# Reading the strided operand on TensorE instead of PSUM on VectorE: the closes of images 1 to 3 of a state-space and attention block

## The chip, the cores and the metric

The kernel runs on one core of one Trainium2 chip. The metric is the device time of a run in microseconds. Before the change three runs took 6413.48, 6416.27 and 6428.01 us, a median of 6416.27 us.

## The reference

The input is four images of 96 channels and 128x128 pixels. Two layers follow each other, each of the form x + layer(groupnorm(x)).

Layer 0 is a state-space block: a projection to 192 channels, a depthwise 3x3 convolution, four scans over the pixels (by rows, by columns, and both backwards), a norm, and a projection back to 96 channels.

Layer 1, in which the change lies, is an attention convolution:

```
xr, x1, x2 = relu_split_norm(x)             # the positive and the negative half, each normalised
y1 = layer_norm(attn_conv(x1, x2))          # softmax(key x query) gives 3x3 weights for each image
y2 = layer_norm(conv3x3(x2, w_conv2)) * x1
out = xr + conv1x1(concat(y1, y2), w_full) + b_full
```

The last line is what the text calls the **close** of an image. Two products of 96x96 with the pixels of the image, one for y1 (called `o` in the kernel) and one for y2 (called `c2`), are summed, and `xr` with the layer's residual (called `e`) is added. The norms are folded in: `o` carries a row of ones for the shift, and `c2` has its mean subtracted and is multiplied by `x1` on VectorE before the product.

## The kernel before

**Stages.** First the state-space block runs for all images, in part beside image 0's layer 1. Then images 0 to 3 go through layer 1 one after the other. `attention` is the convolutions of one image (helpers `products` and `outputs`: matmuls at L1477 and L1492, copies out of PSUM on ScalarE at L1550, combinations on VectorE at L1564 to L1572). Beside the convolutions of image b runs the lighter work: the norm and the splitting of image b+1, and the close of image b-1. Image 3 has nobody after it, so its close is cut up in the class `LastOutput`: `before` prepares `x1` and `e` early, `beside` adds the product of `c2` and `e` into an SBUF tile `kept` beside image 3's own last convolution, and `after` adds the product of `o` at the very end and stores.

**The order of the work.** Python generators yield an estimated cost after each piece, and `co_run` interleaves two of them by these costs: the attention on the left, the lighter chain on the right. The order in which instructions are emitted so is the order on each engine's queue; each engine waits on semaphores for its operands. The costs yielded are constants in the code and do not depend on how long an instruction takes on the chip.

**Two orders of pixels.** Image 0 goes through layer 1 with its pixels in the plain order (row by row); in the code it is `mapped`. Images 1 to 3 are kept with every row of 128 pixels cut into four sets of every fourth pixel (32 each), since their convolution works on such planes. The result has to leave in plain order, so each close of images 1 to 3 must turn it somewhere. Two views of a row do that: `pixels(v)` (L2292) reads a tile of planes in pixel order, so that its last dimension has 4 elements at a step of 32 words; `plain(v)` (L2296) is a tile in pixel order, contiguous, written with the same dimensions.

**The close.** In `attn_output` (L2299) a step is 8 rows of the image, 1024 pixels, 16 steps an image. In a step the tiles `o`, `c2` and `xx` come from DRAM; ScalarE and VectorE make `x1` and `e` (L2283 to L2290), VectorE scales `c2` (L2326), and for each of two halves of 512 pixels TensorE does two matmuls into one PSUM bank (L2334 and L2335), and VectorE adds `e` and writes the output tile (L2337 for image 0, contiguous; L2339 for images 1 and 2, with PSUM and `e` read by `pixels`). The tile is stored by a DMA on SyncE's queue at L2341. `beside` has the same with one matmul (L2412) and the addition at L2413. In `after`, one addition at L2440 takes 1024 pixels from two PSUM banks and adds into `kept` in place; its matmuls are at L2436, its store at L2443, and all 16 steps of it follow the last convolution, with nothing else left to do.

Of the kernel before, what the change touches and what calls it, by code (L numbers as in the profile page):

```python
# [20 lines left out]
CH = 512  # L21
# [50 lines left out]
def kernel(  # L72
# [26 lines left out]
    nc = tc.nc  # L99
# [236 lines left out]
    def traced():  # L336
        return nc.cur_bb.bb.instructions

    def in_order(first):


        before = {}
        for i in traced()[first:]:
            if i.engine in before:
                tc.add_manual_dep(
                    i,
                    before[i.engine].name,
                    mybir.DependencyInfo(
                        mybir.DependencyClass.NoSync, mybir.DependencyReason.DATA
                    ),  # L350
                    reason="order of emission",
                )
            before[i.engine] = i
# [56 lines left out]
    def image_stats(b, pool):  # L410
# [17 lines left out]
        return mv, run  # L428

    def project(b, weights, mv, beside, zb, xrows, ps):  # L430


# [1019 lines left out]
    def pairs_of(ps):  # L1452

        return ps.tile([128, 2, CH], F32, name="two", tag="two")
# [804 lines left out]
    def own_weights(img, ps, pool):  # L2259

        so, _ = combine(ps, img.ost.rearrange("p c s -> p (c s)"), mean96, "so")
        ro = col("ro")
        rsqrt(ro, so[:, 1:2])
        w1 = pool.tile([128, C], F32, name="w1")
        nc.vector.tensor_scalar(w1[0:C], wful[:, 0], ro, None, ALU.mult)
        nso = col("nso")
        nc.vector.tensor_scalar(nso, so[:, 0:1], -1.0, None, ALU.mult)
        pt = bank(ps)[C : C + 1, 0:C]  # L2270
        nc.tensor.matmul(pt, lhsT=img.keep["low"][:, 1:2], rhs=ident, start=True, stop=False)
        nc.tensor.matmul(pt, lhsT=nso, rhs=w1[0:C], start=False, stop=True)  # L2272
        nc.vector.tensor_copy(w1[C : C + 1], pt)
        return w1[0 : C + 1]

    def with_ones(pool, name, bufs=None):
        y = pool.tile([128, SN], F32, name=name, tag=name, bufs=bufs)
        nc.gpsimd.memset(y[C : C + 1], 1.0)
        return y[0 : C + 1]

    def first_half(img, xx, x1):
        thr, scale, shift = (img.keep[n] for n in ("thr", "scale", "shift"))
        nc.scalar.activation(x1, xx, AF.Identity, scale=scale[:, 0:1], bias=shift[:, 0:1])  # L2283
        nc.vector.scalar_tensor_tensor(x1, xx, thr, x1, ALU.is_gt, ALU.mult)

    def residual(img, xx, e):
        up, low, thr = (img.keep[n] for n in ("up", "low", "thr"))
        nc.scalar.activation(e, xx, AF.Identity, scale=up[:, 0:1], bias=up[:, 1:2])
        nc.vector.scalar_tensor_tensor(e, xx, thr, e, ALU.is_gt, ALU.mult)
        nc.vector.scalar_tensor_tensor(e, xx, low[:, 0:1], e, ALU.mult, ALU.add)  # L2290

    def pixels(v):  # L2292

        return v.rearrange("p (h j t) -> p h t j", j=TW, t=TN)

    def plain(v):  # L2296
        return v.rearrange("p (h t j) -> p h t j", j=TW, t=TN)

    def attn_output(img, ps, side, share):  # L2299
        ob = out[img.b].rearrange("c h w -> c (h w)")  # L2300
        with (
            tc.tile_pool(name="f1", bufs=1, side=side) as p1,
            tc.tile_pool(name="f3", bufs=2, side=side) as p3,
        ):
            w1 = own_weights(img, ps, p1)
            s2, w2 = c2_weights(img, ps, p1)
            ones = [with_ones(p1, f"o{i}") for i in range(2)]

            def loads(t):
                o = ones[t % 2]  # L2310
                got = [o]
                nc.sync.dma_start(o[0:C], img.od[:, bass.ts(t, SN)])
                for name, src in (("c2", img.c2d), ("xx", img.xnew)):
                    y = p3.tile([C, SN], F32, name=name)
                    nc.sync.dma_start(y, src[:, bass.ts(t, SN)])
                    got.append(y)
                return got

            ahead = loads(0)
            for t in range(NS):  # L2320
                o, c2, xx = ahead
                if t + 1 < NS:
                    ahead = loads(t + 1)
                x1 = p3.tile([C, SN], F32, name="x1")
                first_half(img, xx, x1)
                nc.vector.scalar_tensor_tensor(  # L2326
                    c2, c2, s2[0:C, 0:1], x1, ALU.subtract, ALU.mult
                )
                e = p3.tile([C, SN], F32, name="e")
                residual(img, xx, e)  # L2330
                for h in range(2):
                    sl = bass.ts(h, CH)
                    pf = part(ps, C, CH)
                    nc.tensor.matmul(pf, lhsT=w1, rhs=o[:, sl], start=True, stop=False)  # L2334
                    nc.tensor.matmul(pf, lhsT=w2, rhs=c2[:, sl], start=False, stop=True)  # L2335
                    if img.mapped:
                        nc.vector.tensor_add(x1[:, sl], pf, e[:, sl])  # L2337
                    else:
                        nc.vector.tensor_add(plain(x1[:, sl]), pixels(pf), pixels(e[:, sl]))  # L2339
                    yield 2.6 * share  # L2340
                nc.sync.dma_start(ob[:, bass.ts(t, SN)], x1)  # L2341

    class LastOutput:
# [38 lines left out]
        def beside(self):  # L2382

            img = self.img
            while self.kept is None:
                yield None
            with (
                tc.tile_pool(name="f1", bufs=1, side=self.side) as p1,
                tc.tile_pool(name="f3", bufs=2, side=self.side) as p3,
            ):  # L2390
                s2, w2 = c2_weights(img, self.ps, p1)

                def loads(t):
                    got = []
                    for name, src in (("c2", img.c2d), ("x1", self.x1d), ("e", self.ed)):
                        y = p3.tile([C, SN], F32, name=name)
                        nc.sync.dma_start(y, src[:, bass.ts(t, SN)])
                        got.append(y)
                    return got

                ahead = loads(0)
                for t in range(NS):
                    c2, x1, e = ahead
                    if t + 1 < NS:
                        ahead = loads(t + 1)
                    nc.vector.scalar_tensor_tensor(
                        c2, c2, s2[0:C, 0:1], x1, ALU.subtract, ALU.mult
                    )
                    for h in range(2):
                        sl = bass.ts(h, CH)  # L2410
                        pf = part(self.ps, C, CH)
                        nc.tensor.matmul(pf, lhsT=w2, rhs=c2[:, sl], start=True, stop=True)  # L2412
                        nc.vector.tensor_add(  # L2413
                            plain(self.kept[:, t, sl]), pixels(pf), pixels(e[:, sl])
                        )
                        yield 2.2

        def after(self, pairs):

            img, ob = self.img, out[self.img.b].rearrange("c h w -> c (h w)")  # L2420
            with (
                tc.tile_pool(name="f1", bufs=1, side=self.side) as p1,
                tc.tile_pool(name="f3", bufs=6, side=self.side) as p3,
            ):
                here = (H - OWN) // RS
                loaded = []
                for t in range(here):
                    o = with_ones(p3, "o")
                    nc.sync.dma_start(o[0:C], img.od[:, bass.ts(t, SN)])
                    loaded.append(o)  # L2430
                w1 = own_weights(img, self.ps, p1)
                for t in (*range(here, NS), *range(here)):
                    o = loaded[t] if t < here else self.own[0 : C + 1, bass.ts(t - here, SN)]
                    pf = pairs_of(pairs)[:C]
                    for h in range(2):
                        nc.tensor.matmul(  # L2436
                            pf[:, h], lhsT=w1, rhs=o[:, bass.ts(h, CH)], start=True, stop=True
                        )
                    to = self.kept[:, t]
                    nc.vector.tensor_add(  # L2440
                        plain(to), pixels(pf.rearrange("p h w -> p (h w)")), plain(to)
                    )
                    nc.sync.dma_start(ob[:, bass.ts(t, SN)], to)  # L2443
                    yield 2.6

# [252 lines left out]
```

## Time and profile before

| What | Value |
|---|---|
| median of 3 runs | 6416.27 us |
| profiled execution, its own time | 6409.68 us |
| its span in the profile | 6407.8 us |
| mean granted TensorE clock | 0.902 |
| DMA, mean over the span | 188 GB/s |
| close of image 1: VectorE's additions at L2339 | 5461 to about 5672 us |
| close of image 2: the same | about 5680 to 5907 us |
| image 3, `beside`: additions at L2413 | 6205 to 6349 us |
| image 3, `after`: matmuls at L2436 | 6366 to 6397 us |

One execution was profiled. The span counts from the first to the last event of the profile, and the execution's own time is 1.9 us longer. "PE" is TensorE's matmul, "PEld" its loading of weights, which overlaps; "DVE" is VectorE, "ACT" ScalarE, "POOL" GpSimd. A matmul of f32 in the code is two instructions of each kind in the profile. The matmuls are pipelined, so the duration of one includes its latency, and two in a row start closer together than they last. A row of a group has the line in the kernel, engine, operation, output and inputs, shapes and count, and then the busy time and the mean of one in ns, or the minimum, median and maximum.

### The profile page before, as it was taken

The page shows a single profiled execution, that of the slowest core. Times are in us where ns is not written, and L with a number is a line of the kernel's source. Part 1 is how long each engine was busy: PE and PEld are TensorE (multiplying, and loading weights), DVE is VectorE, ACT ScalarE, POOL GpSimd, SP SyncE. Part 2 cuts the span into 40 slices and gives each one's busy share as a digit, 9 for nine tenths or more (in the row PEclk, how much of TensorE's full clock was granted, in tenths as well). Part 3 has the DMA queues.
Part 4 walks back from the last instruction along what each step waited for, and adds up shares of the span by engine and source line. Part 5 has one row for each costly group of instructions (what it writes and reads, how often), then busy time and mean ns, then how long its engine had stood idle before and what let it go on. Part 6 is the DMA issues. An engine that isn't in the chain of part 4 may idle for free. (4 is left out here: it accounts for less than half of the span.)

```text
span 6407.8 us, 76468 instructions
## 1 busy us (share of the span) xinstructions
PE 5253.4 (82%) x23264; PEld 2254.8 (35%) x23264; DVE 4699.9 (73%) x7132; ACT 3759.4 (59%) x4770; POOL 3238.6 (51%) x2476
## 2 busy tenths in 40 slices
PE   6889988987888643989988588977888877889888
PEld 2333322322222111444433234345333444345553
DVE  4247878988989768989844686468774687988767
ACT  1247767787787666777622465466644665545642
POOL 1326757978879554979822234436304365022310
PEclk9899989998999765999999799989989888999989
DMA  6766777775675766676667686665776656967668
GB/s 155 175 160 189 198 199 199 214 221 163 198 202 171 202 183 207 196 213 179 182 185 195 166 228 163 195 169 156 214 199 184 175 149 165 245 167 180 191 168 221
DMA packets 897706, 1205.30 MB, mean 188 GB/s; under 512 B 230644, under 2 KB 745642, under 8 KB 884816
## 3 DMA queue, kind: packets, MB, share of 16 engines
q1 hardware_dynamic: 866640, 1145.36, 65.5%
q0 software_dynamic: 16336, 38.51, 2.3%
q10 hardware_dynamic: 14320, 16.54, 0.9%
q8 instruction: 187, 3.06, 0.2%
q14 instruction: 223, 1.83, 0.1%
HBM read 777.82 MB, written 345.62 MB: 175 GB/s over the span
## 5 line engine op out<-in xcount | busy, mean ns | idle before, releaser
L633 PE MATMUL bank<-y,wp 128*128 128x512 f32 (+3 forms) x3584 | 1310.9, 622 | 83.8 <-DMA y<-y 41.0
L866 POOL TENSOR_TENSOR y<-y,dl 128x1024 f32<-128x1024 f32 x384 | 1058.5, 2757 | 263.0 <-DVE dl L858 240.3
L833 POOL TENSOR_TENSOR dl<-dl,u 128x1024 f32<-128x1024 f32 x384 | 1008.8, 2627 | 253.1 <-ACT dA L809 121.1
L854 DVE TENSOR_TENSOR_SCAN dA<-dA,pBC 128x512 f32<-128x512 f32 x768 | 981.6, 1278 | 30.7
L2169 PE MATMUL bank<-y,wn 128*64 128x384 f32 (+5 forms) x2408 | 680.1, 507 | 58.3 <-DMA y<-x1d 34.1
L1477 PE MATMUL two<-ya,wd 128*64 128x192 f32 (+3 forms) x2376 | 582.2, 414 | 174.0 <-ACT odd L1550 65.1
L633 PEld LDWEIGHTS bank<-y,wp 128*128 128x128 f32 (+3 forms) x3584 | 456.2, 168 | 749.3 <-issue 651.1
L858 DVE TENSOR_TENSOR dl<-dA,pBC 128x512 f32<-128x512 f32 x768 | 528.5, 688 | 255.8 <-PE pBC L747 183.8
L747 PE MATMUL pBC<-xr,wbc 60*128 60x512 bf16 (+1 forms) x1536 | 457.8, 404 | 311.5 <-DVE dA L854 239.1
L1938 ACT COPY yb<-ya 64x768 f32<-64x768 f32 (+1 forms) x660 | 537.7, 815 | 195.5 <-PE two L1477 113.8
L676 ACT ACTIVATE dl<-pd,dtb 128x512 f32<-128x512 f32 x768 | 485.5, 684 | 187.9 <-PE pd L747 171.5
L1477 PE MATMUL two<-yb,wd 128*64 128x192 f32 (+3 forms) x2376 | 559.0, 400 | 4.0 <-ACT yb L1938 4.0
L837 DVE TENSOR_TENSOR pBC<-dl,pBC 128x512 f32<-128x512 f32 x768 | 527.5, 687 | 8.8 <-POOL dl L833 7.8
L2169 PEld LDWEIGHTS bank<-y,wn 128*64 128x64 f32 (+3 forms) x2408 | 310.3, 169 | 357.2 <-issue 186.2
L809 ACT ACTIVATE dA<-dl,negA 128x1024 f32<-128x1024 f32 x384 | 420.3, 1141 | 2.3
L1477 PEld LDWEIGHTS two<-ya,wd 128*64 128x64 f32 (+1 forms) x2376 | 262.2, 165 | 370.9 <-ACT odd L1550 75.0
L676 ACT ACT_TABLE_LOAD x248 | 318.2, 1283 | 91.9 <-PE pd L747 79.7
L747 PEld LDWEIGHTS <-wbc 60*128 60x128 bf16 (+1 forms) x1536 | 103.1, 96 | 752.1 <-issue 739.3
L1477 PEld LDWEIGHTS two<-yb,wd 128*64 128x64 f32 (+1 forms) x2376 | 289.7, 167 | 150.5 <-issue 42.1
L1477 PE MATMUL two<-ya,wa 128*96 128x384 f32 (+1 forms) x528 | 231.2, 521 | 72.9 <-DMA ya<-vp 27.0
L1550 ACT COPY odd<-two 128x384 f32<-128x384 f32 (+5 forms) x176 | 115.8, 658 | 291.3 <-PE two L1492 179.1
L1406 POOL TENSOR_TENSOR pl<-x 96x256 f32<-96x256 f32 (+3 forms) x396 | 275.2, 710 | 0.0
(322 smaller groups left out, 9105.4 us busy)
## 6 DMA issues: line engine op xcount, KB each, us to landing
u<-zb SPq DMA_DIRECT2D x192, 1024.0 KB
yms<-y SPq DMA_DIRECT2D x96, 512.0 KB
xn<-xnew SPq DMA_DIRECT2D x128, 384.0 KB
ya<-vp SPq DMA_DIRECT2D x120, 336.0 KB
y<-y SPq DMA_DIRECT2D x128, 258.2 KB
zb<-z SPq DMA_DIRECT2D x64, 512.0 KB
y<-yms SPq DMA_DIRECT2D x64, 512.0 KB
ya<-x1p SPq DMA_DIRECT2D x90, 336.0 KB
```

The source lines that it names most:

```text
L633: nc.tensor.matmul(blocks(pz[p:e]), lhsT=ws[k][:, d, c : c + e - p], rhs=window(ys[k], at, d, n), start=(i == 0), stop=(i == len(terms) - 1),)
L676: nc.scalar.activation(dst, src, AF.Softplus, bias=bias)
L747: nc.tensor.matmul(p, lhsT=w[rows], rhs=xr[rows, at : at + CH], start=True, stop=True)
L809: nc.scalar.activation(live[m]["dA"], live[m]["dl"], AF.Exp, scale=negA[:, g % 3, k : k + 1])
L833: nc.gpsimd.tensor_mul(t, t, u_view(n))
L837: nc.vector.tensor_mul(p, live[n]["dl"][:, bass.ts(half, CH)], p)
L854: nc.vector.tensor_tensor_scan(h, h, p, init, ALU.mult, ALU.add)
L858: nc.vector.tensor_mul(live[n]["dl"][:, sl], live[n]["dA"][:, sl], live[n]["C", half])
L866: nc.gpsimd.tensor_add(v, v, t.rearrange("p (a b) -> p a b", b=W))
L1477: nc.tensor.matmul(of(to[p:e], r), lhsT=w[:, i, c : c + e - p], rhs=tiles(t[k][PAIR[i]][:, SLOT[i]], o, r), start=(k == 0), stop=False,)
L1938: nc.scalar.copy(yb[k][64 * h - 64 : 64 * h, :, :n], ya[k][0:64, :, h * TN : h * TN + n])
L2169: nc.tensor.matmul(pc[p:e, :n].rearrange("p (h w) -> p h w", w=W), lhsT=w[:, c : c + e - p], rhs=v[:, :, 0:W], start=(i == 0), stop=(i == ...
```

## The change

In the closes of images 1 to 3, the matmuls now read their moving operand (`o` and `c2`, in SBUF) through `pixels`, so that the product stands in PSUM in pixel order. VectorE's addition then reads PSUM through `plain`, in contiguous rows. `e` is still read through `pixels` at L2339 and L2413. In `after`, `kept` is in pixel order already, so the addition becomes contiguous in all its operands and needs no view. Image 0 and everything before the closes stay as they were, and so do the counts of instructions, the tiles, their buffers, the waits and the transfers.

```diff
@@ attn_output
                     pf = part(ps, C, CH)
-                    nc.tensor.matmul(pf, lhsT=w1, rhs=o[:, sl], start=True, stop=False)
-                    nc.tensor.matmul(pf, lhsT=w2, rhs=c2[:, sl], start=False, stop=True)
+                    to, in_order = pf, lambda v: v
+                    if not img.mapped:
+                        to, in_order = plain(pf), pixels
+                    nc.tensor.matmul(to, lhsT=w1, rhs=in_order(o[:, sl]), start=True, stop=False)
+                    nc.tensor.matmul(to, lhsT=w2, rhs=in_order(c2[:, sl]), start=False, stop=True)
                     if img.mapped:
                         nc.vector.tensor_add(x1[:, sl], pf, e[:, sl])
                     else:
-                        nc.vector.tensor_add(plain(x1[:, sl]), pixels(pf), pixels(e[:, sl]))
+                        nc.vector.tensor_add(plain(x1[:, sl]), plain(pf), pixels(e[:, sl]))
@@ LastOutput.beside
-                        nc.tensor.matmul(pf, lhsT=w2, rhs=c2[:, sl], start=True, stop=True)
+                        nc.tensor.matmul(
+                            plain(pf), lhsT=w2, rhs=pixels(c2[:, sl]), start=True, stop=True
+                        )
                         nc.vector.tensor_add(
-                            plain(self.kept[:, t, sl]), pixels(pf), pixels(e[:, sl])
+                            plain(self.kept[:, t, sl]), plain(pf), pixels(e[:, sl])
                         )
@@ LastOutput.after
                         nc.tensor.matmul(
-                            pf[:, h], lhsT=w1, rhs=o[:, bass.ts(h, CH)], start=True, stop=True
+                            plain(pf[:, h]), lhsT=w1, rhs=pixels(o[:, bass.ts(h, CH)]),
+                            start=True, stop=True,
                         )
                     to = self.kept[:, t]
-                    nc.vector.tensor_add(
-                        plain(to), pixels(pf.rearrange("p h w -> p (h w)")), plain(to)
-                    )
+                    nc.vector.tensor_add(to, pf.rearrange("p h w -> p (h w)"), to)
```

## The prediction

> **What bounds the kernel now.** I read the page first, then the groups by line and shape, then the chain of waits, then busy time by stage, then single instructions in order of time. The page's head says TensorE is the busiest engine and VectorE the next; neither is at its limit over the whole span, so the change has to be priced in the stages that it touches.
>
> ```profile
> span 6407.8 us, 76468 instructions
> PE 5253.4 (82%) x23264; PEld 2254.8 (35%) x23264; DVE 4699.9 (73%) x7132; ACT 3759.4 (59%) x4770; POOL 3238.6 (51%) x2476
> ```
>
> Those stages, in the view of busy time by stage (columns: stretch and length, busy time and instructions of PE, PEld, DVE, ACT, POOL, granted clock, DMA share, GB/s), are the close of image 1, the close of image 2, image 3's half with `w2`, and image 3's last half:
>
> ```profile
> 5455.00:5675.00 220.00, 193.97 (x672) 83.30 (x672) 191.26 (x260) 108.91 (x129) 8.79 (x15) 0.93 0.81 219
> 5675.00:5908.00 233.00, 212.25 (x1202) 113.57 (x1198) 193.40 (x264) 110.93 (x134) 68.85 (x84) 0.97 0.69 178
> 6203.00:6349.00 146.00, 135.63 (x425) 55.41 (x426) 111.19 (x157) 59.63 (x74) 0.06 (x1) 0.95 0.86 222
> 6366.00:6398.00 32.00, 31.12 (x64) 11.34 (x64) 19.10 (x17) 0.00 (x0) 5.68 (x6) 0.89 0.68 205
> ```
>
> TensorE is busy 88%, 91%, 93% and 97% of them, VectorE 87%, 83%, 76% and 60%. So here TensorE leads, with VectorE close behind only in image 1's close. The chain of waits ends with the last half, and it is all TensorE:
>
> ```profile
> 6365.90 0.28 DVE w L2273
> 6366.18 0.04 issue
> 6366.23 31.13 PE two L2436 x64
> 6397.36 0.02 issue
> 6397.38 1.22 DVE e L2440
> ```
>
> **VectorE's price of a stride.** One row for each of the forms concerned (minimum, median and maximum ns, first and last start):
>
> ```profile
> L2337 DVE TENSOR_TENSOR x<-bank,e x32: 677/684/689, 4654.1 to 4777.2; 96x512 f32<-96x512 f32 x32
> L2339 DVE TENSOR_TENSOR x<-bank,e x64: 1010/1034/1084, 5461.2 to 5905.8; 96x512 f32<-96x512 f32 x64
> L2440 DVE TENSOR_TENSOR e<-two,e x16: 1221/1221/1221, 6370.0 to 6397.4; 96x1024 f32<-96x1024 f32 x16
> L1570 DVE TENSOR_TENSOR two<-ends,two 96x768 f32<-96x768 f32 x40 | 38.3, 957 | 1.1
> ```
>
> L2337 is the addition with everything contiguous, L2339 the same with PSUM and the SBUF operand `e` both read at a step of 32 words, L2440 with PSUM alone at that step. L1570 takes 957 ns for rows of 768, and 555 ns in its form of 128x384: 1.047 ns an element and 153 ns fixed. A contiguous row of 1024 would then take 1225 ns; L2440 takes 1221. So the PSUM step costs VectorE nothing here, and the 350 ns that L2339 has over L2337 (0.68 ns an element, 1.73 ns in all) belong to `e`, which the change leaves as it is.
>
> **TensorE's pace.** In the last half, in order of time, three loads of weights in a row:
>
> ```profile
> 6387.31 0.16 PEld L2436 LDWEIGHTS two<-o,w 97*96 97x96 f32 x1 [0.27 <-issue]
> ...
> 6387.74 0.16 PEld L2436 LDWEIGHTS two<-o,w 97*96 97x96 f32 x1 [0.27 <-issue]
> 6388.17 0.16 PEld L2436 LDWEIGHTS two<-o,w 97*96 97x96 f32 x1 [0.27 <-POOL o L2278]
> ```
>
> Steady matmuls start 0.43 us apart: 512 columns at 0.84 ns. (The 592 ns of a row is one matmul's length with its latency; the starts are what counts.) Each f32 matmul of the code is two such instructions: L2436 has 64 for 16 steps of 2.
>
> [...]
>
> **The change part by part.** No instruction is added, removed or moved, no DMA changes, no wait is added, and the tiles and their buffers stay. Only the length of existing instructions can change.
>
> VectorE: 64 additions at L2339 and 32 at L2413 lose the step on PSUM and keep it on `e`. Worth 0 by L2440[...], 350 ns each (33.6 us) if, against L2440, the whole excess were PSUM's. [...] The 16 at L2440 become contiguous: 1221 to 1225, nothing. A loss is excluded, since all three streams are at most as scattered as now.
>
> TensorE: in images 1 and 2, 16 steps x 2 halves x 2 matmuls x 2 instructions = 128 each, 256 in all (L2334, L2335); 64 at L2412; 64 at L2436. None of the trace's matmuls moves an operand one word at a time, so the cost is bounded. Below: 0 [...] I take the price that SBUF charges VectorE for exactly this pattern, 1.73 ns a word: 886 ns against 428, +458 each. That is an estimate, carried over from another engine.
>
> TensorE time: 256 x 0.458 = 117 us in the closes; 64 x 0.458 = 29 us at L2412; at L2436 the first 8 instructions start 0.85 us apart, at half the clock, where 1.66 ns a word is the pace anyhow, so 56 x 0.458 = 26 us. Sum 172 us.
>
> What is on the path: in the two closes TensorE is idle 26 and 21 us, part of it latency at the ends of bursts; I let half, 23 us, absorb. Behind a slow matmul stand the convolution's matmuls of the next image in the same queue, and behind those ScalarE's copies and VectorE's combinations, so the rest shows: +94. At L2412 half of 10 us idle absorbs: +24. In the last half nothing hides: +26. But the stores there are behind already:
>
> ```profile
> 6386.00:6396.00 10.00, 10.00 (x25) 3.85 (x24) 7.03 (x7) 0.00 (x0) 1.33 (x2) 1.00 0.94 300
> 6396.00:6400.00 4.00, 1.34 (x4) 0.22 (x2) 2.11 (x2) 0.00 (x0) 0.00 (x0) 1.00 0.95 299
> 6400.00:6404.00 4.00, 0.00 (x0) 0.00 (x0) 0.00 (x0) 0.00 (x0) 0.00 (x0) 0.55 0.95 290
> ```
>
> The DMA engines are full for 20 us, the last addition ends at 6398.6, its store is issued only at 6401.4, and the span ends at 6407.8. A slower TensorE lets that queue run dry and the last store goes at once: about 4 us back, +22 net. Sum +140[...]. The profiled execution took 6409.7 us (span 6407.8), so 6549; the median of the runs lies 6.6 above it, so 6555.
>
> **The rivals.**
> - *TensorE reads the step for free.* For it: the transposes at L1770 load their weights from the ring at a step of 3 words, and lone words cost nothing there: ten in a row take 0.90 us, or 0.083 us for 90 columns, 0.92 ns a word against VectorE's 1.73. [...] It decides if the starts stay 0.43 us apart.
> - *A part of the price.* [...]
> - *A dearer step*[...]
> - *Faster: TensorE reads for free and VectorE's excess was PSUM's.* 96 x 0.35 = 33.6 us of VectorE; where it is the second-busiest engine some half would show, 17 us: 6399. L2440 speaks against it. It decides from 13 us saved, 135 ns an addition.
>
> **How the numbers follow.** A measurement of this kernel tells about 0.2%, 12.8 us, from no change. Chances: full price 0.50, part 0.14, dearer 0.07, free 0.25, faster 0.04. So slower 0.71, same 0.25, faster 0.04. The likeliest is 6555, by itself 6520 to 6590 (absorption of none or of all idle time, a price of 1.6 to 1.8 ns). The range must reach the free case and leaves out the dearer one, the faster one and edges: 6408 to 6590.
>
> **What would show it.** Right: L2334, L2335, L2412 and L2436 start 0.85 to 0.9 us apart in bursts; the last half grows from 31 to about 57 us; the closes are about 47 us longer each; VectorE's L2339 and L2413 stay between 1015 and 1035 ns, L2440 at 1221; the stores after the last addition end sooner than 9.2 us. Wrong: starts still 0.43 us apart (free), or L2339 near 684 ns (the excess was PSUM's)[...]. If the starts double and the closes hardly lengthen, the absorption is what I mis-sized: VectorE, or the DMA at 0.81 of its capacity in image 1's close, would then have been the bound.

## The result and the profile after

The changed kernel takes 6569.57 us, the median of four runs (6567.35 to 6580.81), against 6414.88 us before (four runs, one more than in the table above). The ratio is 1.0247 with a 95% interval of 1.0229 to 1.0266: slower by 155 us between the medians, by 158 us by the ratio. The profiled execution has a span of 6565.5 us, 157.7 more than the one of before, so the two traces can be compared stretch by stretch.

The page of the kernel after, its head:

```profile
span 6565.5 us, 76455 instructions
PE 5449.6 (83%) x23264; PEld 2286.2 (35%) x23264; DVE 4705.9 (72%) x7132; ACT 3765.0 (57%) x4770; POOL 3237.1 (49%) x2476
```

TensorE is busy 196 us longer with the same number of instructions. VectorE, for whose sake PSUM is now read in rows, is busy 6 us longer. The forms that answer to those of before (minimum, median and maximum in ns; L2338 was L2335 and holds image 0's close too, L2342 was L2339, L2415 was L2412, L2418 was L2413, L2441 was L2436, L2446 was L2440):

```profile
L2338 PE MATMUL bank<-c,w x192: 590/1047/1169, 4649.6 to 6011.0; 96*96 96x512 f32 x192
L2415 PE MATMUL bank<-c,w x64: 1032/1048/1093, 6310.6 to 6479.2; 96*96 96x512 f32 x64
L2441 PE MATMUL two<-o,w x64: 1047/1047/1167, 6504.0 to 6558.9; 97*96 97x512 f32 x64
L2342 DVE TENSOR_TENSOR x<-bank,e x64: 1010/1031/1085, 5461.2 to 6012.1; 96x512 f32<-96x512 f32 x64
L2418 DVE TENSOR_TENSOR e<-bank,e x32: 1010/1028/1052, 6312.7 to 6480.3; 96x512 f32<-96x512 f32 x32
L2446 DVE TENSOR_TENSOR e<-two,e x16: 1219/1221/1221, 6507.8 to 6560.0; 96x1024 f32<-96x1024 f32 x16
```

A matmul with the strided operand lasts 1047 ns where it lasted 592, and VectorE's additions have lost 3 to 7 ns of 1035, or nothing. The distance from one start to the next is shorter than that length: in the last half, in order of time, the loads of weights now start 0.87 us apart instead of 0.43:

```profile
6540.68 0.26 PEld L2441 LDWEIGHTS two<-o,w 97*96 97x96 f32 x1 [0.61 <-issue]
6541.55 0.26 PEld L2441 LDWEIGHTS two<-o,w 97*96 97x96 f32 x1 [0.61 <-issue]
6542.42 0.26 PEld L2441 LDWEIGHTS two<-o,w 97*96 97x96 f32 x1 [0.61 <-issue]
```

This half alone would not tell the price of the step from that of the clock, which was 0.50 throughout: before the change the contiguous matmuls at half the clock started 0.85 us apart as well. L2415 tells it. In its stretch the clock averaged 0.89, and not one of its 64 matmuls took less than 1032 ns, where the median before was 592 ns at 0.94.

The chain of waits ends as before with TensorE's last half, 56.02 us instead of 31.13:

```profile
6503.99 56.02 PE two L2441 x64
6560.01 0.02 issue
6560.03 1.22 DVE e L2446
```

Where the 157.7 us lie is seen by cutting both traces at the same three instructions: the first addition of image 1's close, the first matmul beside image 3's convolution, and the first matmul of the last half. The first of them starts at 5461.2 us in both traces. Busy time by stretch (length, then PE, PEld, DVE, ACT, POOL, clock, DMA share, GB/s), of before:

```profile
5461.00:6204.00 743.00, 651.87 (x3733) 357.83 (x3731) 586.88 (x887) 382.22 (x471) 166.34 (x239) 0.94 0.71 190
6203.90:6366.20 162.30, 142.39 (x457) 59.13 (x456) 124.54 (x187) 62.91 (x81) 5.41 (x6) 0.94 0.82 214
6366.20:6407.80 41.60, 31.12 (x64) 11.34 (x64) 19.54 (x16) 0.00 (x0) 5.68 (x6) 0.83 0.69 209
```

and of after:

```profile
5461.00:6310.60 849.60, 775.92 (x3732) 374.86 (x3730) 588.92 (x886) 382.11 (x470) 165.56 (x239) 0.90 0.62 166
6310.60:6504.00 193.40, 177.16 (x458) 63.46 (x457) 125.13 (x187) 62.85 (x81) 5.41 (x6) 0.89 0.70 180
6504.00:6565.50 61.50, 55.99 (x64) 16.22 (x64) 19.53 (x16) 0.00 (x0) 5.68 (x6) 0.50 0.48 141
```

The stretches grow by 106.6, 31.1 and 19.9 us. In the first, image 1's close (its last addition starts at 5652 us before, not at 5672, and at 5698 us after) is 46 us longer and image 2's 61. Two things are to be seen beside the lengths. The granted clock fell in each (0.94 to 0.90, 0.94 to 0.89, 0.83 to 0.50). And VectorE, ScalarE and GpSimd did the same work in the same time: they only waited longer.

### The profile page after: what moved, and what is told of

The parts are those of the page before. It is cut to its first block, busy times and chain, and to the rows that moved or that the text cites. A ratio compares the mean times of both kernels' runs of the same rounds, so it can differ in the third digit from the quotient of the medians.

```text
span 6565.5 us, 76455 instructions
## 1 busy us (share of the span) xinstructions
PE 5449.6 (83%) x23264; PEld 2286.2 (35%) x23264; DVE 4705.9 (72%) x7132; ACT 3765.0 (57%) x4770; POOL 3237.1 (49%) x2476
## 5 line engine op out<-in xcount | busy, mean ns | idle before, releaser
L1477 PE MATMUL two<-ya,wd 128*64 128x192 f32 (+3 forms) x2376 | 597.3, 424 | 163.8 <-ACT odd L1550 65.4
L1477 PE MATMUL two<-yb,wd 128*64 128x192 f32 (+3 forms) x2376 | 569.2, 407 | 4.0 <-ACT yb L1938 4.0
L1477 PEld LDWEIGHTS two<-ya,wd 128*64 128x64 f32 (+1 forms) x2376 | 268.3, 170 | 377.1 <-issue 92.8
L1477 PEld LDWEIGHTS two<-yb,wd 128*64 128x64 f32 (+1 forms) x2376 | 295.8, 171 | 164.1 <-issue 54.5
L1550 ACT COPY ends<-two 128x384 f32<-128x384 f32 (+5 forms) x176 | 116.1, 660 | 326.0 <-PE two L1492 278.1
```

The costliest lines, as they stand in the source:

```text
L1477: nc.tensor.matmul(of(to[p:e], r), lhsT=w[:, i, c : c + e - p], rhs=tiles(t[k][PAIR[i]][:, SLOT[i]], o, r), start=(k == 0), stop=False,)
```

## The experiments

Each kernel below is set against runs of the unchanged kernel from its own session: 27 with a median of 6411.34 us for the first four, 19 with 6407.07 us for the last four.

My theory (A in the expectations): TensorE reads a lone word in 1.7 ns (0.87 us for 512, at the granted clock of 0.50 above), and as slowly at the full clock, and nearly all of that time lies on the path. The rivals: the loss comes from elsewhere (B), a gain of VectorE is hidden in it (C), or much of it is the lower clock (D).

**The three places one by one.** Each of the next three kernels takes the change in one place only. First the closes of images 1 and 2, both matmuls and the addition:

```diff
-                    nc.tensor.matmul(pf, lhsT=w1, rhs=o[:, sl], start=True, stop=False)
...
+                    to, in_order = pf, lambda v: v
+                    if not img.mapped:
+                        to, in_order = plain(pf), pixels
+                    nc.tensor.matmul(to, lhsT=w1, rhs=in_order(o[:, sl]), start=True, stop=False)
...
```

> Only the closes of images 1 and 2 are changed; image 3's close stays as before. Theory A (TensorE reads a lone word per 1.7 ns, and nearly all of that time lies on the path): 256 instructions x 0.44 us = 112 us less a little absorbed, the 106 us by which the two closes are longer in the profile after; +100 to +112 us, about 6521 us. Rival B (the step itself is partly hidden, and much of the loss comes from elsewhere, such as later stages being disturbed): under +80 us.

Measured: 6524.33 us, ratio 1.0178 (1.0154 to 1.0202), 114 us slower.

Then the half beside image 3's convolution:

```diff
-                        nc.tensor.matmul(pf, lhsT=w2, rhs=c2[:, sl], start=True, stop=True)
+                        nc.tensor.matmul(
+                            plain(pf), lhsT=w2, rhs=pixels(c2[:, sl]), start=True, stop=True
+                        )
...
```

> Only the half of image 3's close that runs beside its last convolution is changed. Theory A: +26 to +31 us, about 6444 us (64 instructions x 0.44 us = 28 us, and in the profile after the stretch from its first matmul to the last half is 31 us longer). Rival B: under +15 us. The three parts, this one and the two others, should add up to the whole change, +155 us, within 10 us under A.

Measured: 6436.91 us, ratio 1.0045 (1.0026 to 1.0064), 29 us slower.

Then the last half:

```diff
-                            pf[:, h], lhsT=w1, rhs=o[:, bass.ts(h, CH)], start=True, stop=True
+                            plain(pf[:, h]), lhsT=w1, rhs=pixels(o[:, bass.ts(h, CH)]),
+                            start=True, stop=True,
...
```

> Only the last half of image 3's close is changed, with nothing beside it. Theory A: the matmuls grow from 31 to 56 us (+25), and 5 us come back because the stores no longer lag: +20 us, about 6435 us. Without the return of the stores +25. In the profile, the time from the end of the last addition to the end of the span falls from 9.2 to about 4.3 us.

Measured: 6437.15 us, ratio 1.0038 (1.0021 to 1.0054), 24 us slower. In the trace of this kernel the last half, cut as above, is:

```profile
6381.40:6443.00 61.60, 56.16 (x64) 16.30 (x64) 19.53 (x16) 0.00 (x0) 5.68 (x6) 0.50 0.47 141
```

61.6 us against 41.6, so the matmuls' 25 us and the stores' return of 5 are both there. The three sum to 167 us against 158 for the whole (by the medians 164 against 155), which their intervals (plus or minus 11 to 15 us each) allow. Rival B falls: the loss is made in each of the three places, in the proportion of the traces.

**VectorE's half alone.** TensorE reads contiguously, VectorE reads PSUM in rows, in all three places:

```diff
-                        nc.vector.tensor_add(plain(x1[:, sl]), pixels(pf), pixels(e[:, sl]))
+                        nc.vector.tensor_add(plain(x1[:, sl]), plain(pf), pixels(e[:, sl]))
...
```

> VectorE's half of the change alone: it reads PSUM in contiguous rows in the closes of images 1 to 3, while TensorE reads its operand contiguously as before, so the product is added in the wrong order of pixels; the amount of work is the same. Theory A (the step of 32 words in PSUM costs VectorE nothing): L2339 and L2413 stay at 1015 to 1035 ns, the time within 0.2% of before. Rival C (the excess of these additions was PSUM's, and the change has a gain of VectorE in it that the loss on TensorE covers): the additions fall to about 690 ns and the time by about 17 us.

Measured: 6414.9 us, ratio 1.0008 (0.9996 to 1.0019). Its additions:

```profile
L2339 DVE TENSOR_TENSOR x<-bank,e x64: 1007/1036/1078, 5457.1 to 5901.8; 96x512 f32<-96x512 f32 x64
L2413 DVE TENSOR_TENSOR e<-bank,e x32: 1015/1035/1055, 6201.1 to 6343.4; 96x512 f32<-96x512 f32 x32
```

The medians are within 2 ns of the 1034 and 1035 of before. Rival C falls: in these kernels reading PSUM at a step of 32 words costs VectorE nothing, with `e` at that step beside it (1034 ns with the step, 1036 without) as well as alone (1221 ns with and without). The excess over a contiguous addition (684 ns) is `e`'s; in the last kernel below, where `e` is contiguous too, it is gone (687 ns).

**The same TensorE time without the step.** In the closes of images 1 and 2 each matmul, that with `w1` and that with `w2`, is issued twice, read contiguously:

```diff
-                    nc.tensor.matmul(pf, lhsT=w1, rhs=o[:, sl], start=True, stop=False)
+                    for again in range(1 if img.mapped else 2):
+                        nc.tensor.matmul(
+                            pf, lhsT=w1, rhs=o[:, sl], start=(again == 0), stop=False
+                        )
...
```

> The operand is read contiguously as before, but in the closes of images 1 and 2 each matmul is issued twice (the product then counts twice in the output): 256 more instructions at full pace, 256 x 0.428 us = 110 us of TensorE, nearly what the step adds there. Theory A (what counts is TensorE's time, and hardly any is absorbed): +95 to +110 us, as in the run with only the two closes changed. Rival D (a good part of that run's loss is the clock, which was granted at 0.88 in the second close instead of 0.97 while TensorE streams at half rate): clearly less, +60 to +85 us, with the clock of the closes at 0.95 or more.

Measured: 6462.96 us, ratio 1.0084 (1.0065 to 1.0103), only 54 us slower. This missed theory A, and went below rival D's numbers. The first stretch of this kernel, cut as above:

```profile
5465.00:6265.00 800.00, 743.17 (x3987) 395.12 (x3985) 586.38 (x887) 386.59 (x472) 159.81 (x239) 0.95 0.66 176
```

With the close's own matmuls in the same stretch, those that read the tile `w`, the three kernels come apart so (busy time counts matmuls that overlap once; the rows of the two matmuls overlap here, so they are taken together):

| first stretch, us | before | after | twice |
|---|---|---|---|
| length | 743 | 850 | 800 |
| the close's own matmuls, busy | 130 | 230 | 231 |
| all other matmuls, the rest of the busy time | 522 | 546 | 512 |
| TensorE idle | 91 | 74 | 57 |

The own time added is nearly the same, +100 and +101. But the other matmuls, the same ones and as many, take 24 us longer after the change and 10 us less here. The 24 us are longer matmuls: the commonest large form of the convolution, 128x384 at L1477 from `ya`, 240 in the stretch in each kernel, lasts 518 ns on average before, 541 after and 521 here, and the lengths of all the others together, overlaps counted in full, are 1322, 1370 and 1324 us. The 10 us less are not shorter matmuls, then, but matmuls that stand closer together. The convolution's largest line shows the loss too, 871 of its matmuls during the two closes (PE and PEld busy, clock, DMA share, GB/s), before and after:

```profile
5461.00:5906.00 445.00, 207.69 (x872) 110.10 (x872) 0.95 0.75 197
```

```profile
5461.00:6012.00 551.00, 225.41 (x871) 120.04 (x872) 0.89 0.60 159
```

and here the clock during the closes is 0.98 to 1.00:

```profile
5465.60:5669.00 203.40, 198.16 (x576) 80.11 (x575) 168.22 (x208) 92.78 (x104) 1.56 (x2) 1.00 0.78 211
5669.00:5949.00 280.00, 272.55 (x1442) 139.22 (x1440) 205.19 (x301) 120.48 (x146) 59.56 (x88) 0.98 0.60 159
```

So rival D holds in part: during the two closes the granted clock averaged 0.89 with the strided read and 0.98 to 1.00 with the contiguous matmuls issued twice, and the other matmuls on TensorE lasted longer in the first (541 against 521 ns in the form above). The clock changes in these traces in steps of 3.4 us. Take the steps during the two closes that had the full clock and were filled to nine tenths or more by the closes' own matmuls: after the change 9 of 16 were followed by a step at half the clock, with only the closes changed 11 of 18, with the contiguous matmuls issued twice 0 of 19. The lower clock went together with the strided read; what sets the granted clock, no run shows. Of the 50 us between the two kernels 24 are slower matmuls; 10 are the closer matmuls here and 17 the idle time that went here, less 1 of own time. For these last two there is a reservation: the 256 new instructions also changed the order on the queues in this kernel, so how much of them went for that reason stays open. The changed kernel has the instructions of VectorE, ScalarE and GpSimd in the order of before.

**What a word costs by its step.** Two kernels in which the four places read at other steps. The first has step 2 in image 1's close, 4 in image 2's, 8 beside image 3's convolution, and `runs(..., 2, 16)` in the last half:

```diff
+    def step(v, s):
+        return v.rearrange("p (a s) -> p s a", s=s)
...
+    def runs(v, n, k):
+        return v.rearrange("p (a k n) -> p k a n", k=k, n=n)
...
-                    nc.tensor.matmul(pf, lhsT=w1, rhs=o[:, sl], start=True, stop=False)
...
+                    if img.b == 1:
+                        to = pf.rearrange("p (s a) -> p s a", s=2)
+                        ra, rb = step(o[:, sl], 2), step(c2[:, sl], 2)
...
+                    nc.tensor.matmul(to, lhsT=w1, rhs=ra, start=True, stop=False)
...
```

> What does a word cost TensorE by its step? The moving operand is read at other steps, and the order of pixels comes out wrong for it; VectorE is as before. Image 1's close reads at a step of 2 words (8 bytes), image 2's at 4 words (16 bytes), the next half at 8 words, and the last half in pairs of adjacent words that hop 32 words. [...] step 2 and the pairs free, 0.43 us from start to start; step 4 and step 8 full price, 0.86 us. Word theory (any word not adjacent to the last costs[...]): step 2 already at 0.86 us and the pairs free. Step theory (only long hops cost): pairs cost too, 0.64 us or more.

The second has `thirds` in image 1's close, step 16 in image 2's, 128 beside, and `runs(..., 4, 8)` in the last half:

```diff
+    def thirds(v, h):
+        return v[:, 128 * h : 128 * h + 768].rearrange("p (a s) -> p s a", s=3)[:, 0:2]
...
```

> The same with other steps: image 1's close reads at a step of 3 words (12 bytes, as the transposes read their weights without a price), image 2's at 16 words (64 bytes), the next half at 128 words (512 bytes), and the last half in runs of 4 adjacent words that hop 32 words. [...] steps 16 and 128 at 0.86 us; runs of 4 free. Word theory: step 3 at 0.86 us. [...]

The times of the whole were 6518.23 and 6503.93 us, of one run each; the argument rests on the length of the matmuls at each place. Of the first kernel (image 1 at step 2, image 2 at 4, beside at 8, last half in hopping pairs):

```profile
L2350 PE MATMUL bank<-o,w x60: 610/612/1061, 5458.0 to 5634.8; 97*96 97x512 f32 x60
L2350 PE MATMUL bank<-o,w x56: 1062/1079/1195, 5699.7 to 5968.5; 97*96 97x512 f32 x56
L2428 PE MATMUL bank<-c,w x64: 1080/1097/1137, 6280.9 to 6455.2; 96*96 96x512 f32 x64
L2455 PE MATMUL two<-o,w x64: 591/592/1169, 6476.1 to 6506.2; 97*96 97x512 f32 x64
```

Of the second (step 3, step 16, step 128, and runs of four):

```profile
L2350 PE MATMUL bank<-o,w x60: 838/844/1061, 5444.3 to 5639.6; 97*96 97x512 f32 x60
L2350 PE MATMUL bank<-o,w x56: 1019/1034/1169, 5705.5 to 5963.1; 97*96 97x512 f32 x56
L2428 PE MATMUL bank<-c,w x64: 1031/1047/1092, 6267.4 to 6436.7; 96*96 96x512 f32 x64
L2455 PE MATMUL two<-o,w x64: 592/592/1169, 6461.4 to 6491.7; 97*96 97x512 f32 x64
```

Over the 592 ns of a contiguous read, 512 words at a step of 2 cost 20 ns more, of 3 252, of 4 487, of 8 505, of 16 442, of 32 (the change) 455 and of 128 455. Pairs and runs of four that hop 32 words cost nothing, though they are read through views with as many dimensions as the change's, so it isn't the form of the view either. The word theory falls with step 2, the step theory with the pairs and with step 4. What came true are the numbers that each expectation names first: step 2, the pairs and the runs of four free or nearly so, steps 4, 8, 16 and 128 near the full price. In time a word, reckoned from these lengths and the 0.84 ns of the contiguous read, step 3 takes 0.84 + 252/512 = 1.33 ns (its starts are 0.67 to 0.68 us apart in the trace, between free and full price) and step 32 takes 0.84 + 455/512 = 1.73 ns. So in these runs the price rises with the step from 2 to 4 words and hardly changes from there to 128, and it vanishes where each hop brings two or four adjacent words. Why it does so, they don't show.

**A third way.** Could the turn be had without either stride, on ScalarE? Here are the closes; beside image 3's convolution the copy goes into `kept`:

```diff
-                        nc.vector.tensor_add(plain(x1[:, sl]), pixels(pf), pixels(e[:, sl]))
+                        nc.vector.tensor_add(e[:, sl], pf, e[:, sl])
...
+                if not img.mapped:
+                    nc.scalar.copy(plain(x1), pixels(e))
...
```

> A version that turns neither on TensorE nor on VectorE: in the closes of images 1 and 2 and in the half of image 3's that runs beside its last convolution, VectorE adds in the order of planes, all contiguous, in place into e, and ScalarE, which is half idle there, copies the sum into pixel order, 1024 at a time. VectorE's additions fall from 1035 to about 690 ns, 96 x 0.35 = 33 us less; ScalarE gets 48 copies of 1.3 to 2.0 us. If VectorE's time counts in these stages beside TensorE's: 5 to 17 us faster. If TensorE alone sets them, as theory A has it: within 0.2%, or a little slower by ScalarE's later copies for the convolution.

Measured: 6413.5 us, ratio 1.0012 (0.9997 to 1.0026). The additions fell as expected, and the copies cost 2.0 us each:

```profile
L2339 DVE TENSOR_TENSOR e<-bank,e x64: 668/687/690, 5452.3 to 5898.1; 96x512 f32<-96x512 f32 x64
L2342 ACT COPY x<-e x32: 1967/2004/2068, 5453.8 to 5898.8; 96x1024 f32<-96x1024 f32 x32
```

From the first addition of image 1's close to the last of image 2's it takes 446 us, before 445: 22 us less on VectorE there bought nothing. That fits stages that TensorE sets, with VectorE's stride hidden behind it; that ScalarE's 59 us more (215 to 274 us busy in the two closes) ate up a gain is not excluded. None of the runs points to a version faster than before.

## Why the prediction was right

The prediction was 6555 us, +140 on the profiled execution; the span grew by 157.7. Step by step:

- **VectorE gains nothing.** Right: 1034 to 1031 ns, 1035 to 1028, 1221 to 1221, and the run with VectorE's half alone shows no gain. The comparison of L2440 with L1570 carried it.
- **TensorE's price, 458 ns an instruction, carried over from VectorE.** Right in size: 455. That the price on TensorE is VectorE's within 3 ns was an estimate from another engine that came true, and no run shows why. The rival of a free read fell, and the evidence that I gave for it misled: the weights read at a step of 3 words at L1770 took 0.92 ns a word, but the moving operand at step 3 costs 252 ns in 512 words, 1.33 ns a word, as the second kernel of steps shows.
- **TensorE time in the closes, 117 us.** Too high: the rows show 100 us added. I discounted the instructions that already ran at half the clock only in the last half; the mean of L2335 before, 653 ns in the closes over a median of 592 at a granted clock of 0.95, says that some did there too, which is part of the 17. Beside image 3's convolution 29 us were forecast and 25.3 came (34.5 to 59.8 us busy).
- **Absorbed idle time, 23 us in the closes and 5 beside.** Near: TensorE's idle time fell by 17 us (91 to 74) and by 4 us (19.9 to 16.2).
- **What the sum left out: the clock.** The other matmuls took 24 us longer in the first stretch and 9.5 us beside image 3's convolution (142.4 - 34.5 = 107.9 us to 177.2 - 59.8 = 117.4), with the granted clock at 0.90 and 0.89 instead of 0.94. That makes +107 where I had +94, and +31 where I had +24. I treated TensorE's other matmuls as fixed. That these matmuls slowed is shown by the traces, and that the lower clock went together with the lone words too: in the last half, where only the read differs, the clock stays at 0.50 with them (in two kernels) and averages 0.88 to 0.89 with pairs and runs of four, and with the doubled matmuls it was granted at 0.98 to 1.00 in the closes, against 0.95 before. That the one causes the other is my reading.
- **The last half, +26 and 4 back.** Measured +24.9, and 5.0 back: the span ended 9.2 us after the last addition before, 4.2 us after it now. The backlog of stores that the chain of waits doesn't name was rightly read from the DMA's share.

The error of 18 us has the other matmuls, slower while the clock was lower, as its largest term, +33 us, against 21 us by which I had the matmuls' own time too high in the first two stretches; the smaller terms make up the rest. That the sum came within 18 us is thus in part luck: a cost that I left out and a cost that I had too high offset each other. The range would have held without that.

## What to carry to other kernels

In these kernels a step of 4 to 128 words on TensorE's moving f32 operand brings 512 columns to 0.85 to 0.92 us from start to start (by the loads of weights in the traces: 0.85 at step 16, 0.87 at step 32, up to 0.92 at step 8), where the contiguous read took 0.43 us at the full clock: twice that time, and little more than the 0.85 us that half the clock took with the contiguous read. Reading in pairs of adjacent words cost nothing (592 ns), and at a step of two 20 ns. So a layout like this one is best turned where the read costs nothing (here VectorE's read of PSUM, 1034 ns with the step and 1036 without), and not on the engine that sets the stage. When a change makes matmuls longer, price the other matmuls beside them too, not only those that were changed: here they took 24 and 9.5 us more.

## What was not expected

The clock: in the last half TensorE is busy without a gap for 56 us and is granted 0.50 throughout, where the contiguous read has 1.00 from 10 us on. The lone-word read took the same 0.87 us an instruction at a granted clock of 1.00 (four in a row from 5484.6 us in the trace after, loads of weights at 5484.64, 5485.50 and 5486.37) as at 0.50, so the lower clock cost these strided matmuls nothing; their neighbours took longer (518 to 541 ns in the form of L1477 above). And the price hardly depends on how far the next word is once the step is 4: steps of 4 to 128 words lie between 1034 and 1097 ns, with the longer steps at the lower end.
